# Layers 2 and 3 of a four-layer convolution chain with the image held in units of 16 rows

## Chip, core and metric

The kernel runs on one core of a Trainium2 chip. The metric is the device time in microseconds of one execution, the median of several runs. All data is float32. Engines are named as the profile names them: PE (TensorE) multiplies matrices, DVE (VectorE), ACT (ScalarE) and POOL (GpSimd) work element by element, and SP (SyncE) issues DMAs.

## The reference, cut to what matters

Four images of 192 channels and 64x64 pixels pass through four layers: a deformable convolution with channel attention and an MLP (layer 0), a non-local attention over all pixels (layer 1), an overlapping window attention with a gated MLP (layer 2), and a depthwise convolution whose weights are made from the image's mean (layer 3). The change is in layers 2 and 3:

```python
def _hft(x, w, b):
    a = 3.0 * x
    for s in (2, 4, 8):
        pool = x.reshape(B, C, h // s, s, ww // s, s).mean(axis=(3, 5))
        a = a - jnp.repeat(jnp.repeat(pool, s, axis=2), s, axis=3)
    return jax.nn.sigmoid(_dwconv3(a, w, b)) * x
...
    s_img = _reverse(s, H, W)               # sums of the softmax, folded back
    o_img = _reverse(o, H, W).reshape(B, HEADS, ch, H, W)
    out = (o_img / s_img[:, :, None]).reshape(B, C, H, W)
    out = _hft(_conv1x1(out, proj_w, proj_b), hft_w, hft_b)
    x1 = x + out
    z = jax.nn.gelu(_conv1x1(_ln_c(x1, n2g, n2b), fc1_w, fc1_b), approximate=False)
    z1, z2 = jnp.split(z, 2, axis=1)
    z = z1 * _dwconv3(_ln_c(z2, sgn_g, sgn_b), sg_w, sg_b)
    return x1 + _conv1x1(z, fc2_w, fc2_b)
...
# layer 3: weights from the mean, four of nine taps (above and left) are kept
    pooled = x.mean(axis=(2, 3))
    t = jax.nn.relu(gamma * (pooled @ w1.T - running_mean) * rsqrt(running_var + EPS) + beta)
    wt = (t @ w2.T + b2).reshape(b * DIM, 1, K, K) * MASK
    out = depthwise_conv(x, wt) + bias
```

## The kernel before, in words

The four images go through the same stages one after the other, and parts of the next image's layer 0 are woven in between.

- **Layer 0.** `offsets` (from L327; L449 computes the offsets) and `gather` (L539 to L557) do the deformable convolution; `mlp0` (L654 to L815) does the attention product and the MLP in 33 steps, four for each of eight chunks of 8 rows and one ahead. Its image is held with channels 0-127 on 128 partitions and 128-191 in halves of 64 partitions.
- **Layer 1.** `keys` (loads L826, transposes L829, products L834, copies L837) makes the keys of an image, and `layer1` (L841 to L960) is the large attention: products L881, L947. The `gather` of the next image is woven into it.
- **Layer 2, windows.** `windows` (L964 to L1182) does the attention in 8x8 windows with a stride of 6, eleven rows of eleven windows. Windows are taken in pairs. `outputs` adds each window's values into an image row by products (L1132) and, by one more product per window, the sums of the softmax (L1137): its moving operand is a piece of the identity, 64 columns.
- **Layer 2, project.** `project` (L1295 to L1359) takes the image in eight chunks of 8 rows, each as two halves of 96 channels on 96 partitions. `first(i)` does the projection (PE L1312, ACT L1315), the pooling sums by pairs (DVE L1323, L1326), their scaling (L1329), the sum of the levels (L1334), and writes a strip with a border of one pixel (ACT L1339, DVE L1345); POOL copies border rows between strips (L1266, L1267). `second(i)` does nine depthwise taps per half on DVE (L1290, L1292), a sigmoid on ACT (L1352), a product (L1354) and the add to x (L1355). For the last image five of the nine taps go to PE (L1284).
- **Layer 2, mlp.** `mlp` (L1361 to L1498) is written out by hand in a fixed order, ten iterations for eight chunks. In an iteration `widen` makes six products of 128 channels (L1387) with a gelu each (L1390), in two groups of three; the norm of the next chunk and the norm of the gate (L1398 to L1420) run between; `taps_of` does the nine gate taps of the chunk two before on DVE (two of them on PE for the last image); `narrow` multiplies back to 192 channels (L1438); `end` adds to x (L1445).
- **Layer 3.** `layer3` (L1500 to L1573) makes four weights per channel from the sums, and then for eight pieces of 8 rows and two halves each: one tap on ACT (L1562), three on DVE (L1571), a store (L1572). For the last image a part of the pieces is done on PE (L1557).
- **The weaving in `rest`.** `project`, `mlp` and `layer3` are generators. The number that each yields is added to a credit, and for each whole credit one step of the next image's `mlp0` is emitted. The yields of `project` sum to 12, of `mlp` to 19, of `layer3` to 4; 33 are used. What is left is emitted at the end. After `rest` come `keys(b+1)`, with `offsets(b+2)` woven in, and `layer1(b+1)`. For the last image there is no such neighbour. PSUM banks of tag "h" are five in `rest`, three for the last image.

Outside `mlp` a scheduler orders the instructions of each engine by its own costs, within the program's dependences. Loads and stores are issued on SP's queue in the order of the program.

Of the kernel before, what the change touches and what calls it, by code (L numbers as in the profile page):

```python
# [10 lines left out]
F32 = mybir.dt.float32  # L11
# [11 lines left out]

M, Q = 128, 64
NCH = 8
CN = HW // NCH
HN = CN // 2
HEADS = 6
# [33 lines left out]
]  # L62
_V96_ONE = ["l1_gb", "l1_thetab", "l1_phib"]
# [10 lines left out]
def conv_seq_kernel(ctx: ExitStack, tc: tile.TileContext, a, out: bass.AP):  # L74
# [22 lines left out]
    V = {}  # L97
# [10 lines left out]
    def halves_of(name, src, pool):  # L108

        t = pool.tile(list(src.shape), F32, tag=name, name=name)  # L110
        nc.sync.dma_start(out=t, in_=src)
        return t
# [24 lines left out]
    for j in range(4):  # L137
        nc.gpsimd.memset(spread[32 * j : 32 * j + 1, j, :], 1.0)
    eps = const([128, 1], "eps")
# [3 lines left out]
    for i in range(3):  # L143
# [4 lines left out]
        thetaT, phiT, gT, wW, qkvT, bias, v48, headsel, sel6, fc1_dram, fc1_bias, fc1b_dram, fc1b_bias, outb, bfc2,  # L148
    ) = (None for _ in range(15))
# [10 lines left out]
    def constants():  # L160

        nonlocal thetaT, phiT, gT, wW, qkvT, bias, v48, headsel, sel6, fc1_dram, fc1_bias, fc1b_dram, fc1b_bias, outb, bfc2
# [39 lines left out]
        bfc2 = const([M, 2], "bfc2")  # L202
        at = 2 * sum(n for _, n in _V96[: [name for name, _ in _V96].index("l0_bfc2")])
        for k, rows, to, of in ((0, P, 0, 0), (0, M - P, P, 1), (1, Q, 0, 1), (1, Q, Q, 1)):
            c = M - P if k == 1 else 0
            in_turn(nc.sync.dma_start(out=bfc2[to : to + rows, k : k + 1], in_=a["v96"][c : c + rows, at + of : at + of + 1]))
# [448 lines left out]
    def mlp0(b, m2, pool, sb, ps):  # L655
# [3 lines left out]
        fc1 = pool.tile([M, 2, 4 * C], F32, tag="fc1", name=f"fc1_{b}")  # L659
        nc.sync.dma_start(out=fc1[0:P, 0, :], in_=fc1_dram[:, 0, :])  # L660
        nc.sync.dma_start(out=fc1[P:M, 0, :], in_=fc1_dram[0 : M - P, 1, :])
        for q in range(2):
            nc.sync.dma_start(out=fc1[Q * q : Q * q + Q, 1, :], in_=fc1_dram[M - P :, 1, :])
# [94 lines left out]
        for i in range(NCH):  # L758
# [25 lines left out]
            def narrow(k):  # L784
# [11 lines left out]
                nc.vector.scalar_tensor_tensor(to, p, bfc2[:, k : k + 1], to, ALU.add, ALU.add)  # L796
# [167 lines left out]
    def windows(b, oi, load_image):  # L964
# [3 lines left out]
        with ExitStack() as s:  # L968
# [151 lines left out]
            def outputs(wr, pair, wins, v, et, sums):  # L1120
# [3 lines left out]
                for i, w in enumerate(wins):  # L1124
# [4 lines left out]
                    for e in range(3):  # L1129
# [6 lines left out]
                    pixels = ident[:, bass.ts(i, 64)].rearrange("p (r c) -> p r c", c=WS)[:, :, d0:d1]  # L1136
                    nc.tensor.matmul(  # L1137
                        to[P : P + HEADS, 0], lhsT=sums[:, pair, :], rhs=pixels, start=first, stop=last,
                        skip_group_check=True,
                    )  # L1140
# [130 lines left out]
    def depthwise(strip, w, k, diag, taps, acc, ps, name):  # L1271


        parts = strip.shape[0]

        def src(tap):
            return strip[:, k, tap // 3 : tap // 3 + 8, tap % 3 : tap % 3 + W]

        to = acc.rearrange("p (r c) -> p r c", c=W)
        last = None  # L1280
        if taps:
            p = ps.tile([128, CN], F32, tag="t", name=name)[:parts]
            for j, tap in enumerate(taps):
                nc.tensor.matmul(p, lhsT=diag[:, k, j, :], rhs=src(tap), start=j == 0, stop=j == len(taps) - 1)  # L1284
            last = p.rearrange("p (r c) -> p r c", c=W)
        for tap in range(9):
            if tap in taps:
                continue
            if last is None:
                nc.vector.tensor_scalar_mul(to, src(tap), w[:, k, tap : tap + 1])  # L1290
            else:
                nc.vector.scalar_tensor_tensor(to, src(tap), w[:, k, tap : tap + 1], last, ALU.mult, ALU.add)  # L1292
            last = to

    def project(b, x, oi, ps, taps, ahead):  # L1295


        with ExitStack() as s:
# [3 lines left out]
            hft_diag = diagonals("hft", V["l2_hftw"], 2, taps, s1) if taps else None  # L1302
            get, share = strips(s1.tile([P, 3, 2, 10, W + 2], F32, tag="hft", name=f"hft_{b}"))
            prs = {}

            def first(i):
                pr = sb.tile([P, 2, CN], F32, tag="pr", name=f"pr_{b}_{i}", bufs=3)
                prs[i] = pr
                for h in range(2):
                    p = ps.tile([128, CN], F32, tag="h", name=f"pp_{b}_{i}_{h}")[:P]  # L1310
                    for k in range(2):
                        nc.tensor.matmul(  # L1312
                            p, lhsT=projT[:, k, bass.ts(h, P)], rhs=oi[:, k, bass.ts(i, CN)], start=k == 0, stop=k == 1
                        )
                    nc.scalar.activation(pr[:, h, :], p, AF.Identity, bias=V["l2_projb"][:, h])  # L1315

                sums = [pr.rearrange("p k n -> p (k n)").rearrange("p (r c) -> p r c", c=W)]
                for lev in range(3):
# [3 lines left out]
                    t = sb.tile([P, nr // 2, ncol], F32, tag=f"pt{lev}", name=f"pt_{b}_{i}_{lev}")  # L1322
                    nc.vector.tensor_tensor(t, pairs[:, 0], pairs[:, 1], ALU.add)  # L1323
                    pairs = t.rearrange("p r (c e) -> p e r c", e=2)
                    q = sb.tile([P, nr // 2, ncol // 2], F32, tag=f"pq{lev}", name=f"pq_{b}_{i}_{lev}")
                    nc.vector.tensor_tensor(q, pairs[:, 0], pairs[:, 1], ALU.add)  # L1326
                    sums.append(q)
                for lev in range(1, 4):
                    nc.vector.tensor_scalar_mul(sums[lev], sums[lev], 0.25**lev)  # L1329
                for lev in (2, 1):  # L1330
                    fine = sums[lev].rearrange("p (r e) (c f) -> p e r c f", e=2, f=2)
                    coarse = sums[lev + 1]
                    for e in range(2):
                        nc.vector.tensor_tensor(  # L1334
                            fine[:, e], fine[:, e], coarse.unsqueeze(3).to_broadcast(list(coarse.shape) + [2]), ALU.add
                        )
                t = get(i)
                for k in range(2):
                    nc.scalar.activation(  # L1339
                        t[:, k, 1:9, 1 : W + 1], pr[:, k, :].rearrange("p (r c) -> p r c", c=W), AF.Copy, scale=3.0  # L1340
                    )
                    for e in range(2):
                        to = t[:, k, 1 + e : 9 : 2, 1 : W + 1].rearrange("p r (c f) -> p r c f", f=2)
                        mean = sums[1][:, 4 * k : 4 * k + 4, :]
                        nc.vector.tensor_tensor(to, to, mean.unsqueeze(3).to_broadcast([P, 4, 32, 2]), ALU.subtract)  # L1345
                share(i)

            def second(i):
                acc = sb.tile([P, 2, CN], F32, tag="acc", name=f"ha_{b}_{i}")
                for k in range(2):  # L1350
                    depthwise(get(i), V["l2_hftw"], k, hft_diag, taps, acc[:, k, :], ps, f"ht_{b}_{i}_{k}")
                    nc.scalar.activation(acc[:, k, :], acc[:, k, :], AF.Sigmoid, bias=V["l2_hftb"][:, k])  # L1352
                cols = bass.ts(i, CN)
                nc.vector.tensor_tensor(acc, acc, prs.pop(i), ALU.mult)  # L1354
                nc.vector.tensor_tensor(x[:, :, cols], x[:, :, cols], acc, ALU.add)  # L1355
# [414 lines left out]
```

## Time and profile before

| what | us |
|---|---|
| median of three runs | 7190.85 (7181.6 to 7196.93) |
| the profiled execution | 7273.0 |
| its span, first to last instruction | 7271.2 |
| mean granted PE clock in it | 0.921 of full |
| `windows` of the last image | 6495 to 6814 |
| `rest` of images 0, 1, 2, to the last x add or output tap | 1943 to 2502, 3650 to 4209, 5370 to 5929 |
| `rest` of image 3 | 6814 to 7267 |
| `mlp0` of image 0, with nothing beside it | 677 to 873 |

The page of the profile gives each engine's busy time, the chain of work that ended last, and the costliest groups of instructions (line, engine, operation, out<-in with partitions x elements, count; then busy time and mean ns of one; then idle time before them and what ended it). A float32 product appears as two records on PE, each with a weight load (PEld). The trace also gives the busy times of all engines between two times, which is how the stages are read; times are counted from the span's start.

### The profile page before, as it was taken

To read this page: it belongs to the slowest core of one execution; us is meant where nothing else is said; L and a number is where in the kernel's file an instruction comes from. 1 tells how busy PE (TensorE), PEld (TensorE's weight loads), DVE (VectorE), ACT (ScalarE), POOL (GpSimd) and SP (SyncE) were. 2 spreads that over 40 slices of the span, in tenths; PEclk is the share of its full clock that TensorE was granted. 3 is DMA by queue.
4 is the path that set the end of the run, shared out by engine and by line. 5 is a ranking of instruction groups with operands and counts; after the bars stand their busy time and mean duration, and the time that the engine had idled before them with its cause. 6 is when DMAs were issued, how large, how long until landed. Compare 5 with 4: busy or idle time off the path is not lost.

```text
span 7271.2 us, 117763 instructions
## 1 busy us (share of the span) xinstructions
PE 6455.8 (89%) x45792; PEld 4350.1 (60%) x45792; DVE 5104.6 (70%) x8112; ACT 3798.2 (52%) x6375; POOL 2124.8 (29%) x2412
## 2 busy tenths in 40 slices
PE   6677999999978899998978889999997889989987
PEld 3345578875544468885644448886654447766532
DVE  3554289975678759984596849995577867755767
ACT  3554278864443358874544338884443425535332
POOL 2653056742100037761200026773210000002100
PEclk8778999999989899998989889998998979989998
DMA  7785256641000176661010066763010010010000
GB/s 228 250 308 160 79 173 214 218 142 31 23 25 14 58 221 221 215 213 40 8 36 15 17 206 198 222 217 110 12 28 21 12 49 9 14 34 12 2 5 19
DMA packets 357710, 741.41 MB, mean 102 GB/s; under 512 B 45735, under 2 KB 239959, under 8 KB 356382
## 3 DMA queue, kind: packets, MB, share of 16 engines
q0 software_dynamic: 95040, 467.22, 19.9%
q1 hardware_dynamic: 262110, 266.65, 12.4%
q8 instruction: 361, 5.91, 0.3%
q14 instruction: 199, 1.63, 0.1%
HBM read 627.22 MB, written 106.21 MB: 101 GB/s over the span
## 4 chain that ended last, share of the span: by engine, by line
PE 65%; DVE 21%; ACT 4%; issue 3%; DMA 2%; SPq 1%; POOL 0%; another core or an unknown queue 0%; ACTq 0%; DVEq 0%; POOLq 0%
PE s L881 12%; PE y L947 11%; PE h L557 7%; DVE ga L1292 6%; DVE ha L1292 3%; PE v L1107 3%; PE h L1387 3%; PE qk L1032 2%; PE t L1115 2%; PE qk L1033 2%; PE f L1438 2%; PE po L449 2%; PE o L1132 1%; PE pm_l2n L327 1%; PE tp L829 1%
## 5 line engine op out<-in xcount | busy, mean ns | idle before, releaser
L539 POOL DMA_INDIRECT ring<-table,idx x1188 | 1675.6, 1410 | 1159.8 <-DVE row L546 254.5
L881 PE MATMUL s<-ths,ph 96*128 96x256 f32 x4096 | 979.4, 385 | 13.9 <-issue 9.1
L881 PEld LDWEIGHTS s<-ths,ph 96*128 96x128 f32 x4096 | 782.7, 193 | 153.6 <-issue 16.0
L545 ACT ACTIVATE row<-ring,pos 128x384 f32<-128x384 f32 x1188 | 698.5, 610 | 235.2 <-DVE xo L550 146.0
L546 DVE SCALAR_TENSOR_TENSOR row<-ring,fr,row 128x384 f32<-128x384 f32 x1188 | 699.1, 612 | 101.5 <-ACT row L545 67.6
L947 PE MATMUL y<-sc,gx 128*97 128x256 f32 x3008 | 723.4, 379 | 0.0
L549 ACT ACTIVATE xo<-row,pos 128x192 f32<-128x192 f32 x1188 | 506.2, 449 | 163.3 <-remote 57.5
L947 PEld LDWEIGHTS y<-sc,gx 128*97 128x97 f32 x3008 | 489.5, 164 | 123.1 <-issue 1.1
L1292 DVE SCALAR_TENSOR_TENSOR ga<-gate,v,ga 128x512 f32<-128x512 f32 x720 | 541.4, 752 | 28.0 <-DVE ga L1292 0.5
L550 DVE SCALAR_TENSOR_TENSOR xo<-row,fr,xo 128x192 f32<-128x192 f32 x1188 | 464.7, 411 | 134.4 <-ACT xo L549 94.6
L557 PE MATMUL h<-ti,xo 128*128 128x192 f32 x2376 | 464.7, 329 | 5.6 <-DVE xo L550 5.6
L883 ACT COPY sc<-s 128x1024 f32<-128x1024 f32 x376 | 377.2, 1003 | 172.7 <-PE s L881 144.1
L944 DVE TENSOR_TENSOR sc<-sc,mbs 128x1024 f32<-128x1024 f32 x376 | 448.7, 1217 | 12.7 <-ACT mbs L907 11.9
L888 DVE TENSOR_TENSOR top<-top,sc 128x1024 f32<-128x1024 f32 x282 | 344.5, 1222 | 137.7 <-ACT sc L883 116.6
L557 PEld LDWEIGHTS h<-ti,xo 128*128 128x128 f32 x2376 | 405.8, 191 | 42.7 <-DVE xo L550 9.9
L1091 DVE TENSOR_REDUCE es<-ex 128x6 f32<-128x384 f32 x264 | 133.3, 546 | 394.6 <-ACT ex L1087 394.6
L945 ACT ACTIVATE sc<-sc 128x1024 f32<-128x1024 f32 x376 | 393.2, 1054 | 27.3 <-DVE sc L944 18.4
L557 PE MATMUL h<-kept,xo 128*128 128x192 f32 x990 | 264.6, 403 | 123.5 <-DVE xo L550 55.7
L1387 PE MATMUL h<-d_l2n,fc1T 96*128 96x512 f32 x768 | 352.3, 607 | 10.1 <-ACT z L1390 7.8
L1266 POOL COPY gate<-gate 128x192 f32<-128x192 f32 x28 | 12.3, 440 | 1170.4 <-ACT gate L1420 1170.4
L557 PEld LDWEIGHTS h<-kept,xo 128*128 128x128 f32 x990 | 191.3, 226 | 213.3 <-DVE xo L550 85.9
L1292 DVE SCALAR_TENSOR_TENSOR ha<-hft,v,ha 96x512 f32<-96x512 f32 x432 | 304.6, 740 | 3.6 <-POOL hft L1266 2.2
(344 smaller groups left out, 11807.4 us busy)
## 6 DMA issues: line engine op xcount, KB each, us to landing
ti<-table SPq DMA_DIRECT2D x396, 96.0 KB
table<-tt SPq DMA_DIRECT2D x24, 1056.0 KB
ring<-table,idx POOLq DMA_INDIRECT x1188
xnd<-xn SPq DMA_DIRECT2D x4, 3270.0 KB
table<-kept SPq DMA_DIRECT2D x12, 1056.0 KB
table<-tt SPq DMA_DIRECT2D x44, 288.0 KB
xi<-in_x_dram SPq DMA_DIRECT2D x32, 384.0 KB
xk<-xd SPq DMA_DIRECT2D x32, 384.0 KB
```

What stands on the lines that cost most here:

```text
L539: nc.gpsimd.indirect_dma_start(out=gt.rearrange("p r q c -> p (r q c)"), out_offset=None, in_=table[:, :], in_offset=bass.IndirectOffsetOn ...
L545: nc.scalar.activation(row, gt[:, :, 0, :], AF.Copy, scale=pos[:, t, 9 + tap : 10 + tap])
L546: nc.vector.scalar_tensor_tensor(row, gt[:, :, 1, :], fr[:, t, 9 + tap : 10 + tap], row, ALU.mult, ALU.add)
L549: nc.scalar.activation(xo[:, j, :], row[:, 0, :], AF.Copy, scale=pos[:, t, tap : tap + 1])
L550: nc.vector.scalar_tensor_tensor(xo[:, j, :], row[:, 1, :], fr[:, t, tap : tap + 1], xo[:, j, :], ALU.mult, ALU.add)
L557: nc.tensor.matmul(acc[m // 2][:, bass.ts(m % 2, C)], lhsT=xo.rearrange("p j c -> p (j c)")[:, bass.ts(m, 128)], rhs=tt, start=t == 0 and ...
L881: nc.tensor.matmul(p[:, t, :], lhsT=ph[:, bass.ts(G * g + t, 128)], rhs=ths[i], start=True, stop=True)
L944: nc.vector.tensor_tensor(ex, ex, mbs[i].unsqueeze(1).to_broadcast([128, G, QN]), ALU.add)
L945: nc.scalar.activation(ex, ex, AF.Exp)
L947: nc.tensor.matmul(py, lhsT=gx[:, G * g + t, :], rhs=ex[:, t, :], start=g == 0 and t == 0, stop=g == NG - 1 and t == G - 1,)
L1292: nc.vector.scalar_tensor_tensor(to, src(tap), w[:, k, tap : tap + 1], last, ALU.mult, ALU.add)
L1387: nc.tensor.matmul(p, lhsT=fc1b[:, k, bass.ts(m, 128)], rhs=hns[i][:, k, :], start=k == 0, stop=k == 1)
```

## The change

The image of layers 2 and 3 is held as six units of 16 rows and 1024 pixels: units 0 to 3 are channels 0-127 on 128 partitions, units 4 and 5 are channels 128-191, with the upper half of the image on partitions 0-63 and the lower half on 64-127. Elementwise instructions work on a whole unit. Per-channel vectors get the same layout (`VW`), built once by 28 small products. `project` runs by unit, and its depthwise taps become a generator with yields between them. Its pooling levels are summed with a factor of 0.25 in the add, so that the scaling is gone. Between units 4 and 5 the two border rows that cross partitions are moved by DMA.

In `mlp` the chunks stay 8 rows, with 128 channels in one instruction and 64 in a second. `widen` goes over the two channel groups outside and the three outputs inside, so that three banks are open at once. `layer3` runs by unit; unit 4's row above its lower half comes by DMA (`over`). For the last image only unit 1 is on PE.

The yields change: `project` now sums to 22, `mlp` to 16, `layer3` to 0. In `windows` the softmax sums of a pair of windows are added by one product of up to 112 columns, with a constant `pixels`.

```diff
-                    pixels = ident[:, bass.ts(i, 64)].rearrange("p (r c) -> p r c", c=WS)[:, :, d0:d1]
-                    nc.tensor.matmul(
-                        to[P : P + HEADS, 0], lhsT=sums[:, pair, :], rhs=pixels, start=first, stop=last,
-                        skip_group_check=True,
-                    )
+                c0, n, m = STRIDE * wins[0] - PAD, STRIDE * (len(wins) - 1) + WS, 64 * len(wins)
+                d0, d1 = max(0, -c0), min(n, W - c0)
+                nc.tensor.matmul(
+                    pos[wr][P : P + HEADS, 0, :, c0 + d0 : c0 + d1], lhsT=sums[:m, pair, :], rhs=pixels[:m, :, d0:d1],
+                    start=wins[0] == 0, stop=wins[-1] == NWIN - 1, skip_group_check=True,
+                )
...
+    def depthwise_steps(strip, w, diag, taps, acc, ps, name):
...
+        else:
+            nc.vector.tensor_scalar_mul(acc, src(first), w[:, first : first + 1])
+        for j, tap in enumerate(others):
+            nc.vector.scalar_tensor_tensor(acc, src(tap), w[:, tap : tap + 1], acc, ALU.mult, ALU.add)
+            if j % 3 == 1:
+                yield
...
+    def upper_of(x, i):
+        q, at = i // 4, 4 * UN + CN * (i % 4)
+        rows = slice(Q * q, Q * q + Q)
+        return x[:, bass.ts(i, CN)], x[rows, at : at + CN], rows
...
+                if u == 5:
+                    nc.sync.dma_start(out=get(4)[Q:M, 0, row], in_=get(5)[0:Q, UR, row])
+                    nc.sync.dma_start(out=get(5)[0:Q, UR + 1, row], in_=get(4)[Q:M, 1, row])
...
-                for lev in range(1, 4):
-                    nc.vector.tensor_scalar_mul(sums[lev], sums[lev], 0.25**lev)
...
+            for of, u in (
+                (first, 0), (first, 1), (second, 0), (first, 2), (second, 1), (first, 4), (first, 5), (second, 4),
+                (first, 3), (second, 2), (second, 5), (None, 0), (second, 3),
+            ):
+                if of is first:
+                    first(u)
+                    yield 0.33
+                elif of is second:
+                    for _ in second(u):
+                        yield 0.83
+                else:
+                    ahead()
...
+                rows, banks = upper_of(x, i)[2], {}
+                for k, of in ((0, slice(0, M)), (1, rows)):
+                    for m in ms:
+                        if k == 0:
+                            banks[m] = ps.tile([128, CN], F32, tag="h", name=f"h2_{b}_{i}_{m}")
+                        nc.tensor.matmul(
+                            banks[m], lhsT=fc1b[of, k, bass.ts(m, 128)], rhs=hns[i][of, k, :], start=k == 0, stop=k == 1
+                        )
                 for m in ms:
-                    p = ps.tile([128, CN], F32, tag="h", name=f"h2_{b}_{i}_{m}")
-                    for k in range(2):
-                        nc.tensor.matmul(
-                            p, lhsT=fc1b[:, k, bass.ts(m, 128)], rhs=hns[i][:, k, :], start=k == 0, stop=k == 1
-                        )
...
                     if gating:
-                        yield 1.0 if last < 0 else 0.5
+                        yield 1.0 if last < 0 else 0.0
...
+            for u in (0, 1, 2, 4, 3, 5):
...
+                    rows = [(ov[:, a0:], xv[:, r0 - 1 + a0 : r0 + UR - 1])]
+                    if u == 4:
+                        rows.append((ov[:, 0:1], over))
...
+                if k == 0:
+                    nc.sync.dma_start(out=flat[0:M, bass.ts(u, UN)], in_=o)
+                else:
+                    for q in range(2):
+                        at = HW // 2 * q + UN * (u - 4)
+                        nc.sync.dma_start(out=flat[M:C, at : at + UN], in_=o[Q * q : Q * q + Q])
+                yield 0.0
-                nc.sync.dma_start(out=dst[:, :, bass.ts(i, R * W)], in_=o)
-                yield 0.5
```

## The prediction

> **What bounds the kernel now.** I read the page first, its busy shares and the chain that ended last, and then windows of the stages that the change touches.
>
> ```profile
> PE 6455.8 (89%) x45792; PEld 4350.1 (60%) x45792; DVE 5104.6 (70%) x8112; ACT 3798.2 (52%) x6375; POOL 2124.8 (29%) x2412
> ...
> PE 65%; DVE 21%; ACT 4%; issue 3%; DMA 2%; SPq 1%; POOL 0%; another core or an unknown queue 0%; ACTq 0%; DVEq 0%; POOLq 0%
> ```
>
> TensorE (PE) carries the chain as a whole, but most of it in layer 1 (L881, L947), which the change leaves alone. So I cut out the stages, by the table of windows (from:to, length, busy us of PE, PEld, DVE, ACT, POOL, then granted clock, DMA share, GB/s):
>
> ```profile
> 1943.00:2118.00 175.00, 129.54 (x513) 68.84 (x511) 165.52 (x341) 72.09 (x110) 8.44 (x30) 0.83 0.10 28
> 2118.00:2465.00 347.00, 296.74 (x1328) 155.96 (x1328) 264.25 (x371) 132.43 (x193) 9.95 (x42) 0.92 0.06 17
> 2465.00:2614.00 149.00, 131.43 (x925) 68.96 (x925) 66.36 (x101) 54.17 (x98) 11.45 (x14) 0.87 0.56 170
> 5919.00:5975.00 56.00, 55.11 (x162) 36.62 (x163) 14.39 (x24) 6.97 (x10) 3.96 (x5) 0.50 0.26 78
> 6814.00:6925.00 111.00, 107.69 (x266) 41.22 (x266) 99.65 (x220) 36.19 (x53) 12.70 (x47) 0.97 0.02 6
> 6925.00:7190.00 265.00, 219.91 (x838) 102.86 (x836) 177.33 (x224) 93.77 (x119) 10.88 (x35) 0.94 0.01 2
> 6495.00:6814.00 319.00, 289.76 (x5191) 188.70 (x5192) 169.88 (x242) 148.70 (x273) 76.48 (x195) 0.94 0.09 23
> ```
>
> Row 1 is `project` of image 0, with VectorE (DVE) busy 95%. Row 2 is its `mlp`, where neither PE (86%) nor DVE (76%) is full: it is a chain that alternates between them. Row 3 is what follows the last x add: layer 3, keys(1) and offsets(2), PE-bound. Row 4 is keys(3) after image 2, PE 98% busy but at half clock. Rows 5 and 6 are `project` and `mlp` of the last image, with no neighbour: `project` is PE-bound there. Row 7 is a `windows` stage, PE 91%.
>
> **Unit sizes on DVE.** The groups of instructions give a mean per size:
>
> ```profile
> L546 DVE SCALAR_TENSOR_TENSOR row<-ring,fr,row 128x384 f32<-128x384 f32 x1188 | 699.1, 612 | 101.5 <-ACT row L545 67.6
> ...
> L550 DVE SCALAR_TENSOR_TENSOR xo<-row,fr,xo 128x192 f32<-128x192 f32 x1188 | 464.7, 411 | 134.4 <-ACT xo L549 94.6
> ...
> L1292 DVE SCALAR_TENSOR_TENSOR ha<-hft,v,ha 96x512 f32<-96x512 f32 x432 | 304.6, 740 | 3.6 <-POOL hft L1266 2.2
> ```
>
> From 411 ns for 192 elements to 612 for 384: 1.047 ns an element and 210 ns that an instruction costs whatever its size. 512 elements come to 746 (measured 740), 1024 to 1.28 us. [...] The rows (16 x (8 x 0.740 + 0.482) = 102.4, less 6 x (8 x 1.28 + 0.80) = 66.3) make 36. The row is this kernel's own, so I take 36.
>
> **project, images 0 to 2.** DVE's own part falls from 162.8 to about 108.7 us: taps -36, pooling sums (15.4 to 11.6) -4, the scaling of L1329 -5 (folded into the adds), L1345 (13.3 to 9.0) -4, products and x adds (19.4 to 14.6) -5. Alone this would take 175 to about 125. But the new yields sum to 22 credits where the old had 12, so ten more of the 33 steps of the next image's layer-0 MLP (`mlp0`) move in: in the built order five of its eight chunks are before the first widening, not three. Priced at 0.86 us for a 512-column product (two records; the first 16 of L1312 start between 1943.2 and 1949.7 us, 0.43 apart) and half that for 64-row pairs, PE's list grows from 101 to 147.5 us. At a clock of 0.92 that is 160, with waits 167: **-8 each**. Bounds: 147.5 at 0.83, the clock of row 1, is 178 (+3); DVE's 142 plus 8 of waits is 150 (-25). The two row DMAs between units 4 and 5 wait on SyncE for unit 5's strip, and loads of mlp0 stand behind them; PE waited 2.3 us once for such a load in row 1, so a late one costs a few us, within the bounds. POOL's edge copies fall from 14 to six and POOL is idle.
>
> **mlp, images 0 to 2.** The same steps leave here. Six steady iterations, from their first spread to the next, last 36.4, 42.3, 33.6, 44.1, 33.4 us (start times of L1417; mean 38.0): the short ones carry one step of mlp0, the long ones two.
>
> ```profile
> 2206.00:2243.00 37.00, 30.91 (x133) 15.54 (x132) 31.43 (x44) 14.71 (x20) 1.58 (x4) 0.92 0.11 32
> 2243.00:2285.00 42.00, 39.66 (x189) 20.92 (x190) 32.78 (x47) 17.37 (x26) 0.78 (x4) 0.95 0.00 1
> 2285.00:2319.00 34.00, 26.88 (x116) 14.01 (x115) 32.67 (x47) 11.68 (x15) 1.53 (x4) 0.90 0.02 8
> ```
>
> In the second row PE is full, in the third DVE is. With one step each all become the third kind: 38.0 to 34.5, six times, is -21; the end gives 2 more: **-23 each**. DVE is late next, at 32.7 of 34: no removal of mlp0 can bring more than some 10 beyond this. At the other end 0 is gained if the alternation itself sets the time. mlp0 now ends at iteration 8, so keys(b+1) come among the last taps, where DVE is the bound and PE has room; if that cover is missing, eight gx copies of 0.55 us and some 25 us of PE come back. The x adds by 128 and 64 rows are as many as before.
>
> **The tail after the last x add.** Layer 3 is 18 tap instructions of 1.27 us and three short ones on DVE, about 26.5 with buffer waits, after 3.8 for the weights. All output DMAs are now ahead of the next loads on SyncE's queue, so offsets start about 34 us after the last add. Alone at the kernel's start they took 102 (5 to 107 us); I take 98, since their norms need no first loads of constants: 132 against 149, **-17** for images 0 and 1. Bounds: 68, what the part after keys took, gives -47; 102 and a cold clock give +1. After image 2 layer 1 began 83 us after the add; keys are gone, so 34, and 8 for a cold start (its first 28 us now ran at 0.74): **-41**, bounds -49 and -20.
>
> **The clock[...].** Layer 3 with nothing beside it leaves PE idle for some 25 us, and mlp has more gaps. [...] Row 4 says otherwise: 55.11 of 56 us busy, and the clock 0.50 throughout, 28 us lost. [...] by the row they lose up to 60. The start of the kernel[...] had 0.93 over its 102 us, and is nearest to a restart of the same offsets; I keep the figures above.
>
> **The last image.** project: PE's list falls by 8 (pp, 28.6 to 20.6, since the 64-row pairs run side by side) and 18 (ht, 160 records of 72.8 us to 120); DVE's falls to about 70. 111 to 84: **-27**. mlp: only three PSUM banks here, and the new widening fills three at once. In the built order the second and third wait for the x adds on DVE, which are behind a tap, not for a gelu. h3 began at 7036.3, the adds ended at 7044.2; less 3.5 of products that run meanwhile, 4.3 us in each of five iterations: **+21** (0 to +35: DVE idles 5 us there for PE anyway). Layer 3: -2. Sum -8.
>
> **windows.** 121 sums of 64 columns an image become 66, of which 55 have 112. Spacing is 0.21 us for the pair of records at 64 columns and 0.31 at 128 (L1115), so 0.29 at 112: 55 x (0.42 - 0.29) = 7 us of PE, of which 6 show at 91% busy: **-24** for four images (-38 to 0). The 28 small products of the new constants lie in the gather of image 0[...]: 0 (+4 if PE's order delays it).
>
> **Sum.** 3 x (-8 - 23) - 17 - 17 - 41 - 8 - 24 = -200. The profiled execution took 7273.0 (span 7271.2), 1.1% above the median of 7190.85; all differences are made within it. 7190.85 - 200 = **6991**.
>
> **Rivals.** *Less gain* (22%): the woven mlp is latency, not work. Its mean of 38 stays at 36.5 or so (-9 each), project stays at 175 and the keys aren't covered: -27 - 50 - 8 - 24 = about -105, **7085**. For it: neither engine is full in row 2. Against: the periods follow the number of steps. *More gain* (20%): project goes to DVE's 150 (-25 each), the mlp to DVE's 32.7 (-33 each), the tails as above: -75 - 99 - 75 - 8 - 24 = -281, **6910**. *Slower* (5%): the mlp stages, thinned of mlp0, fall to half clock and stay there, as row 4 did. PE's list there is 285 us at full clock now and about 260 after. The stage must end 74 us later than my 324 (three times) to undo the whole: 398. With 25 of waits, 260 over 373 is a clock of 0.70; below that it is slower, at 0.66 about 3 x 20 = 60 us: **7250**. Against it: row 6 is an mlp without mlp0, PE 83% busy, and its clock was 0.94. That the change does not do what it says is excluded by the built order.
>
> **Chances.** Likeliest 53% (6945 to 7040), the rivals as given. A measurement of this kernel tells about 0.2% from no change (14 us). The range takes in both milder rivals in part: 6905 to 7085. Faster 0.94, same 0.02, slower 0.04.
>
> **What would show it.** In the changed profile: `project` near 167 with PE and DVE both about 90% busy; steady mlp iterations all near 34.5; no keys after layer 3; offsets from about 34 us after the last add; the last image's mlp at some 286, with its widenings waiting for x adds. Steady iterations still at 38, or a clock below 0.75 in the second row's place, would prove me wrong.

## The result, and the profile after

The changed kernel takes 7063.4 us (median of four runs, 7056.3 to 7071.5) against 7193.9 us of the kernel before (7181.6 to 7199.6): a ratio of 0.9821, 95% interval 0.9804 to 0.9838, or -130 us. The forecast was 6991 us with a range of 6905 to 7085. A repetition gave 0.9838 (0.9811 to 0.9865).

The profiled execution took 7071.5 (span 7069.4), 202 less than that of before. Of these 202, 77 lie in the first gather, whose code the change leaves as it was: the first MLP product of image 0 (L767 before, L796 after) starts at 614 us, not 692. In all profiles here that start lies between 614 and 692 with either layout; it is late (676 to 688) in the groups of runs where the kernel before takes about 7270, and early (614 to 642) in those where it takes about 7191. So runs of different groups are compared by their ratio to before and stage by stage, and the profile of before is one of the long kind. Without those 77 the two profiles differ by 125.

The engine line of the page after is the one to set beside the first of before:

```profile
PE 6342.5 (90%) x45368; PEld 4236.5 (60%) x45368; DVE 4928.1 (70%) x7476; ACT 3763.7 (53%) x6276; POOL 2122.6 (30%) x2352
```

DVE has 636 instructions fewer and is busy 176 us less. PE is busy 113 us less.

To compare stages I use marks that both traces have: the first projection product, the first widening product, the last x add, the first theta product of the next layer 1. First the windows of before between these marks (`project` and `mlp` of image 0, `mlp` of the last image):

```profile
1943.20:2104.90 161.70, 119.44 (x495) 64.70 (x493) 153.04 (x324) 69.37 (x107) 8.44 (x30) 0.84 0.10 30
2104.90:2465.00 360.10, 306.64 (x1344) 159.91 (x1344) 276.53 (x388) 135.15 (x196) 9.95 (x42) 0.91 0.05 16
6920.30:7239.70 319.40, 247.91 (x885) 112.28 (x884) 217.12 (x283) 96.55 (x122) 10.88 (x35) 0.90 0.01 2
```

and the same three after, with `project` of the last image as the third row:

```profile
1858.60:2026.00 167.40, 158.07 (x767) 89.07 (x766) 136.45 (x206) 83.89 (x123) 5.34 (x16) 0.97 0.17 48
2026.00:2357.40 331.40, 294.44 (x1257) 141.34 (x1256) 257.68 (x365) 124.38 (x178) 12.20 (x43) 0.94 0.06 19
6549.00:6641.50 92.50, 82.38 (x213) 34.24 (x213) 65.57 (x115) 25.53 (x29) 17.10 (x36) 0.93 0.03 7
6641.50:7034.50 393.00, 299.49 (x884) 120.47 (x884) 218.99 (x287) 97.85 (x127) 6.60 (x29) 0.80 0.01 2
```

In `project` PE is now the fuller engine (158 of 167 us busy), and in `mlp` too (294 of 331). The last row is the surprise: the last image's `mlp` has as many PE instructions as before and 52 us more of PE busy time, at a clock of 0.80 instead of 0.90, and is 74 us longer.

| stage | before | after | difference | foreseen |
|---|---|---|---|---|
| project, images 0 to 2 | 161.7 each | 167.4, 166.7, 167.1 | +16 | -24 |
| mlp, images 0 to 2 | 360.2, 360.4, 360.1 | 331.4, 329.3, 327.2 | -93 | -69 |
| last x add to layer 1 | 156.6, 156.8, 82.5 | 142.4, 139.9, 35.8 | -78 | -75 |
| project, last image | 106.1 | 92.5 | -14 | -27 |
| mlp, last image | 319.5 | 393.1 | +74 | +21 |
| layer 3, last image | 31.4 | 34.8 | +3 | -2 |
| windows, four images | 1207.7 | 1192.2 | -15 | -24 |

These stages make -107. The other 18 us lie in `mlp0` and keys of image 0 (-5) and the four layer 1 stages (-13), which the change leaves alone; they were not foreseen. The border between `project` and `mlp` is a matter of the mark: before, the last x add of `project` ends 12.9 us behind the first widening product, after, 14.6 us ahead of it. What can be compared without a mark is the sum of the two: 521.9 to 522.0 before, 498.8, 496.0 and 494.3 after, so -23, -26 and -27 against the -31 foreseen.

What waits in that last `mlp`, by PE's own waits after:

```profile
PE h L1494 <- DVE x L1555: 31.5, 5, 6.3
PE f L1547 <- DVE z L1539: 31.4, 12, 5.7
PE pb_l2n L348 <- DVE r_l2n L1363: 23.5, 7, 3.9
```

The columns are the sum, how often, and the longest. The first line is new: the widening product waits for the x adds, in five iterations, 6.3 us each. That is the wait that the prediction named; but 31.5 us of waiting do not make 74. In four-us slices of one iteration, from the wait on:

```profile
6786.00:6790.00 4.00, 1.16 (x2) 0.64 (x3) 3.38 (x7) 0.00 (x0) 0.00 (x0) 0.68 0.00 0
6790.00:6794.00 4.00, 4.00 (x6) 1.36 (x5) 0.00 (x0) 0.00 (x0) 0.00 (x0) 0.50 0.01 4
6794.00:6798.00 4.00, 4.00 (x6) 1.03 (x4) 0.00 (x0) 1.37 (x2) 0.00 (x0) 0.50 0.00 0
6798.00:6802.00 4.00, 4.00 (x6) 0.99 (x5) 0.00 (x0) 0.69 (x1) 0.00 (x0) 0.50 0.00 0
6802.00:6806.00 4.00, 4.00 (x8) 1.82 (x8) 1.38 (x2) 1.26 (x2) 0.00 (x0) 0.69 0.00 0
6806.00:6810.00 4.00, 4.00 (x11) 1.56 (x10) 1.75 (x1) 1.76 (x2) 0.00 (x0) 1.00 0.00 0
```

After the wait PE is busy without a gap (4.00 of 4), and the granted clock is at 0.50 for 17.1 us (6787.4 to 6804.5). PE gets through six records in four us at first, and eleven once the clock is back. DVE and ACT stand nearly idle meanwhile, since all that they do next hangs on these products.

The five waits are alike, 6.3 us each, but what follows is not: the half clock lasts 20.5, 17.1, 20.5, 6.8 and 13.7 us. Behind the fourth wait the clock is back after four us of work:

```profile
6893.00:6897.00 4.00, 3.61 (x5) 1.27 (x5) 0.99 (x4) 0.00 (x0) 0.00 (x0) 0.54 0.00 0
6897.00:6901.00 4.00, 4.00 (x9) 1.52 (x10) 0.00 (x0) 2.06 (x3) 0.00 (x0) 1.00 0.00 0
```

The iterations with these waits last 52.0, 51.5, 53.0, 45.5 and 45.6 us; the last does less work than the others.

### The profile page after: what moved, and what is told of

Same layout as the page of the kernel before. It is cut to its first block, busy times and chain, and to the rows that moved or that the text cites. A ratio compares the mean times of both kernels' runs of the same rounds, so it can differ in the third digit from the quotient of the medians.

```text
span 7069.4 us, 116083 instructions
## 1 busy us (share of the span) xinstructions
PE 6342.5 (90%) x45368; PEld 4236.5 (60%) x45368; DVE 4928.1 (70%) x7476; ACT 3763.7 (53%) x6276; POOL 2122.6 (30%) x2352
## 4 chain that ended last, share of the span: by engine, by line
PE 45%; DVE 13%; ACT 3%; issue 2%; DMA 1%; POOL 1%; SPq 0%; DVEq 0%; ACTq 0%; POOLq 0%
PE s L910 8%; PE y L976 7%; DVE ga L1324 4%; PE h L590 3%; PE h L1494 3%; PE v L1136 2%; PE qk L1061 2%; PE qk L1062 1%; PE f L1547 1%; PE t L1144 1%; PE po L482 1%; PE zm L1506 1%; PE rb L1210 1%; PE o L818 1%; DVE top L917 1%
## 5 line engine op out<-in xcount | busy, mean ns | idle before, releaser
L572 POOL DMA_INDIRECT ring<-table,idx x1188 | 1696.2, 1428 | 1037.8 <-DMA wkT<-in_wkT_dram 234.6
L910 PEld LDWEIGHTS s<-ths,ph 96*128 96x128 f32 x4096 | 781.8, 192 | 142.4 <-ACT ths L904 16.7
L583 DVE SCALAR_TENSOR_TENSOR xo<-row,fr,xo 128x192 f32<-128x192 f32 x1188 | 465.5, 412 | 40.6 <-ACT xo L582 38.1
L1494 PE MATMUL h<-d_l2n,fc1T 128*128 128x512 f32 (+1 forms) x768 | 375.5, 630 | 34.0 <-DVE x L1555 31.5
L1297 POOL COPY gate<-gate 128x192 f32<-128x192 f32 x28 | 13.9, 497 | 1286.0 <-ACT gate L1528 1286.0
L1494 PEld LDWEIGHTS h<-d_l2n,fc1T 128*128 128x128 f32 (+1 forms) x768 | 143.6, 197 | 252.8 <-issue 189.2
L1547 PE MATMUL f<-z,fc2T 128*64 128x512 f32 (+1 forms) x384 | 222.6, 714 | 74.1 <-DVE z L1539 74.1
```

The source lines that it names most:

```text
L572: nc.gpsimd.indirect_dma_start(out=gt.rearrange("p r q c -> p (r q c)"), out_offset=None, in_=table[:, :], in_offset=bass.IndirectOffsetOn ...
L583: nc.vector.scalar_tensor_tensor(xo[:, j, :], row[:, 1, :], fr[:, t, tap : tap + 1], xo[:, j, :], ALU.mult, ALU.add)
L910: nc.tensor.matmul(p[:, t, :], lhsT=ph[:, bass.ts(G * g + t, 128)], rhs=ths[i], start=True, stop=True)
L1494: nc.tensor.matmul(banks[m], lhsT=fc1b[of, k, bass.ts(m, 128)], rhs=hns[i][of, k, :], start=k == 0, stop=k == 1)
```

## The experiments

Theory 1: the gain of some 200 us is there, less what the last image's `mlp` loses to the wait and to the half clock that it brings. Rivals: the split into 128 and 64 channels costs the time itself; the gain comes from the yields alone and the layout does nothing; the tails are set by the clock.

**Old order of the widening, last image only.**

```diff
-                for k, of in ((0, slice(0, M)), (1, rows)):
-                    for m in ms:
+                both = ((0, slice(0, M)), (1, rows))
+                order = [(k, of, m) for m in ms for k, of in both] if taps else [(k, of, m) for k, of in both for m in ms]
+                for k, of, m in order:
+                    if True:
```

> The changed kernel, with the old order of the widening products (each output's two products together) for the last image only; the other three images keep the new order. Theory 1: the last image's mlp became 74 us longer (319 to 393) because the second and third bank wait for the x adds (6.3 us in each of five iterations) and because PE then runs at half clock for 15 to 20 us (7.7 us more). Both go: mlp about 320, total about 6993. Rival: the 128 + 64 split of norms, adds and products costs the time by its own instructions; mlp stays above 380, total 7050 to 7065.

Measured: 0.9795 (0.9770 to 0.9819); the last `mlp` took 346.6 us, with steady iterations of 40.6 us (52.0, 51.5, 53.0 and 45.5 in the changed kernel, 37.9 before). The wait for the x adds is gone. So the order of the loops is the cause of most of the 74. But 27 us remain against before. The old order has a price of its own, as the PE timeline shows; first this run, then the run below, which keeps the new order. Columns: start, time from the first start to the last end, engine and line, group.

```profile
6864.52 6.29 PE L1496 MATMUL h<-d_l2n,fc1T 128*128 128x512 f32 x12
```

```profile
6828.41 5.51 PE L1494 MATMUL h<-d_l2n,fc1T 128*128 128x512 f32 x12
```

Twelve records take 6.29 us against 5.51. From start to start of two records the trace of the changed kernel has 0.43 us where the records have the same number of rows and come in a row, 0.52 at a change of the number of rows, from 128 to 64 or back, and 0.53 for a second record right behind a change. The new order makes one change of height per three outputs, the old one five. Over the stage the widening products keep PE busy 102.5 us with the old order, 89.9 in the run below and 87.9 before: some 13 to 15 of the 27. Where the rest lies is open. The old order also has the wait of before for a free bank:

```profile
PE h L1496 <- ACT z L1500: 7.8, 10, 0.8
```

**The x adds ahead of the first tap, last image only.**

```diff
+                    if taps:
+                        end()
                     if last >= 0:
                         taps_of(last, 0)
                     end()
```

> The changed kernel, but for the last image the x adds are emitted ahead of the first gate tap of the iteration instead of behind it; the widening keeps its new order. Theory 1: the wait of PE falls from 6.3 us to 2 or less[...], so mlp falls from 393 to about 320 to 330, total about 6995 to 7005. Rival (the split itself costs the time): no change, 7063. If the order of the two loops cost something else than this wait, this run stays clearly above the one with the old order.

Measured: 0.9766 (0.9741 to 0.9791); the last `mlp` 323.1 us, steady iterations 37.3. PE's waits in that stage:

```profile
PE f L1547 <- DVE z L1539: 27.1, 12, 4.5
PE pb_l2n L348 <- DVE r_l2n L1363: 23.5, 7, 3.9
PE pb_z L348 <- DVE rz L1596: 4.6, 1, 4.6
```

The line `PE h <- DVE x` is gone, and with it 70 us of the stage, with all the split instructions in place. The rival that the split costs the time is out. The whole moved by 0.0055 of 7194, some 40 us, not 70. It ran in another group than the changed kernel, one with the longer first gather, and its own layer 1 of image 0 was 19 us longer in the profile; with intervals of 12 and 18 us each way, where the other 30 went stays open.

**Work in the place of the wait.**

```diff
                             banks[m] = ps.tile([128, CN], F32, tag="h", name=f"h2_{b}_{i}_{m}")
+                            for _ in range(7 if taps and m == 3 and 2 < i else 0):
+                                nc.tensor.matmul(
+                                    banks[m], lhsT=fc1b[of, k, bass.ts(m, 128)], rhs=hns[i][of, k, :], start=True, stop=True
+                                )
```

> The changed kernel, and for the last image seven more products with the same operands into the bank of the first output, ahead of the real one, in iterations 3 to 7: about 6 us of work in the place where PE waits. The wait for the x adds stays what it is. If the half clock after the wait costs 7.7 us an iteration as the trace suggests, the period falls from 51 to about 43.5 and the total by about 39, to 7025, although work is added. If the clock is only a symptom and costs nothing on the path, the period stays at 51 and the total at 7063.

Measured: 0.9792 (0.9765 to 0.9818), the stage 360.3 us, steady iterations 43.9 where 43.5 was expected. The same place in an iteration, behind the x adds at 6855.7:

```profile
6852.00:6856.00 4.00, 4.00 (x10) 1.52 (x8) 3.79 (x6) 0.00 (x0) 0.00 (x0) 1.00 0.00 0
6856.00:6860.00 4.00, 3.71 (x9) 1.53 (x9) 1.07 (x4) 0.46 (x1) 0.00 (x0) 1.00 0.00 0
6860.00:6864.00 4.00, 4.00 (x9) 1.27 (x8) 0.64 (x1) 1.60 (x3) 0.00 (x0) 1.00 0.00 0
6864.00:6868.00 4.00, 4.00 (x10) 1.71 (x9) 2.50 (x3) 1.33 (x3) 0.00 (x0) 1.00 0.00 0
```

The clock is 1.00 throughout these 16 us. The five iterations last 44.2, 43.9, 43.9, 43.9 and 39.6 us, so six us of useless products made them shorter by 7.8, 7.6, 9.1, 1.6 and 6.0: least where the changed kernel had its short half-clock stretch of 6.8 us. Added work that shortens an iteration, and most where the half clock was longest, leaves the clock as the only cause. By the whole stage, the clock is 33 us (393.1 to 360.3) and the wait itself 37 (360.3 to 323.1).

**The window sums alone, on the kernel before.** The diff is the part of the change above in `outputs`, with its constant.

> The kernel before, with only the sums of a pair of windows by one product of up to 112 columns (and its constant). Prediction's term: 6 us an image, -24, about 7168. From the trace of the changed kernel: PE's busy time in a windows stage falls by about 12 us at equal clock, but in three of four of its windows stages there is a half-clock stretch of 20 us that before did not have. If this stretch comes with the change of the sums: -10 to -20 in all, about 7178; if not: -40 to -50, about 7148.

Measured: 0.9946 (0.9928 to 0.9964), -39 us, at the upper of the two ends. A windows stage of it, beside 298.1 us and 280.26 of PE before:

```profile
1639.60:1928.40 288.80, 266.40 (x5028) 176.92 (x5027) 165.92 (x235) 144.97 (x268) 70.08 (x192) 0.96 0.10 27
```

PE has 110 records less and 13.9 us less to do, where the prediction had 7. The next rows give the PE and PEld time of the sums alone (first two) and of the value products alone (last two) in that stage, each time before and then this run:

```profile
1645.10:1943.20 298.10, 33.12 (x242) 11.40 (x242) 0.97 0.10 26
1639.60:1928.40 288.80, 22.20 (x132) 6.17 (x132) 0.96 0.10 27
1645.10:1943.20 298.10, 39.48 (x1452) 20.39 (x1452) 0.97 0.10 26
1639.60:1928.40 288.80, 27.58 (x1452) 17.00 (x1452) 0.96 0.10 27
```

(The two kinds overlap in time, so their gains do not add up to 13.9.) So about half of the gain is in products that are as many as before. The likely reason, not tested apart, is that the 64-row value products of two windows now follow each other, where a sum with 128 rows stood between: in the trace of the kernel before, a value product starts 0.15 us behind such a sum (54 times in this stage at full clock), and in that of the changed kernel 0.02 behind the value products of the window ahead. The sums themselves were priced well: from the starts of its records a product of 112 columns takes 0.29 us, one of 64 columns 0.21.

The -39 cannot all be put to this, though. The two profiles differ by 52 us; 35 lie in the windows stages, and 17.6 in the tail of image 2, which this edit leaves alone (its half clock lasted 23.9 us instead of 68.3). And the rival of the expectation came true in the stages: in 31 of the 48 windows stages that were traced with the new sums, a half-clock stretch of 20.5 us or so begins 41 to 43 us into the stage, in none of the eight with the old sums, of which one has a stretch of 54.6 us. With it the new stages take 299.1 us on the mean, without it 291.3, the old ones 297.0 without that one. So the stretch eats most of what the sums save, and their worth lies somewhere between almost nothing and 39 us. It disturbs the pair of profiles above, which shows -15.

**Layout without the yields, and yields without the layout.** In the first, the changed kernel has `yield 0.18` and `0.455` in `project`, 0.5 in `mlp`, 0.667 in `layer3`; in the second, the kernel before has `yield 0.917` and `1.833`, 0.0 and 0.0.

> The changed kernel with its yields scaled to the old sums (project 12, mlp 19, layer 3 four), so that the next image's layer-0 MLP and keys lie where they lay before. Theory: the layout alone frees DVE in project, and the yields move the freed place to the tails. Then project falls to about 131 (from 167), the woven mlp goes back to about 360 (from 331), and the tails come back (78 us in three): together +57 against the changed kernel, ratio 0.990. Rival: the layout is the gain and the yields only shift it about: ratio stays at 0.982.

> The kernel before with only its yields changed to the new sums (project 22, mlp 16, layer 3 none), on the old layout. Theory: project becomes longer (PE's list 154 us over DVE's 163: about 185, +23), mlp shorter by 29, the tails by about 60 in three: -78 in all, ratio 0.989. Rival: without the lighter DVE of the new layout project grows by all that it takes in (+65 each), and the ratio is 1.01 or more.

Measured: 0.9875 (0.9835 to 0.9915) for the layout with the old yields, 0.9913 (0.9885 to 0.9941) for the new yields on the old layout; the changed kernel in the same group 0.9838. `project` and `mlp` of image 0, first with the layout alone:

```profile
1858.40:1988.40 130.00, 110.05 (x495) 60.34 (x493) 116.29 (x177) 60.01 (x85) 4.61 (x16) 0.89 0.13 38
1988.40:2349.30 360.90, 316.39 (x1348) 155.24 (x1344) 272.36 (x384) 138.99 (x204) 9.92 (x42) 0.93 0.05 16
```

then with the yields alone:

```profile
1899.20:2095.80 196.60, 165.30 (x765) 90.96 (x765) 179.77 (x365) 92.40 (x145) 7.13 (x30) 0.93 0.14 41
2095.80:2419.50 323.70, 282.82 (x1237) 145.28 (x1237) 253.59 (x353) 121.84 (x171) 12.15 (x42) 0.92 0.06 16
```

The layout alone takes `project` from 161.7 to 130.0, where DVE is busy 116, and leaves `mlp` as it was. The yields alone make `project` 35 longer and `mlp` 36 shorter, and take 8.4, 8.8 and 38 off the tails. In images 0 and 1 the three stages together are 639 us with the layout alone and 636 to 641 in the changed kernel: with the layout, moving steps from `mlp` into `project` only exchanges the one for the other, since PE is nearly full in both. All that the yields add to the layout is the tail of image 2 (76.2 to 35.9), where keys are the whole of what follows. Against the changed kernel of the same group the three stages make +37, not the +57 of the expectation: the tails of images 0 and 1 came back by 8 us each, not 17.

**PE kept busy in layer 3.**

```diff
+                if not alone:
+                    p = ps.tile([128, CN], F32, tag="h", name=f"warm_{b}_{u}")
+                    for j in range(4):
+                        nc.tensor.matmul(p, lhsT=ident, rhs=o[:, 0:CN], start=True, stop=True)
```

> The changed kernel, with four products that nobody reads after each unit of layer 3 in the first three images, on the unit just finished: PE is busy where it idled some 25 us. In the trace of the changed kernel half clock lasts 44, 44 and 38 us from the start of layer 3, some 20 to 30 of it over the following offsets or layer 1. If PE's idleness causes it: -10 to -13 in each tail, -35 in all, ratio 0.977. If the half clock came with the kind of work (it stood at 0.50 for 56 us of busy PE before): no change, 0.982.

Measured: 0.9824 (0.9795 to 0.9854), no different from the changed kernel. The half-clock stretch at the start of the tails of images 0 and 1 fell from 44 us to two of 14, so PE's idleness is the cause of most of it; but the tails were 144.1, 143.0 and 40.1 instead of 139.7, 139.7 and 35.8. The added products are themselves some 21 us of PE a tail (48 records), so a small gain from the clock could hide behind them; none shows. What the tail waits for is in PE's waits of the changed kernel there:

```profile
PE pm_l L360 <- DMA xi<-in_x_dram: 30.5, 1, 30.5
PE th L902 <- DMA xc<-xd: 6.8, 1, 6.8
```

One load of the next offsets comes 30 us late. It reads the kernel's input, which is there from the start; it stands on SyncE's queue behind the stores of layer 3, and these wait for DVE:

```profile
SPq L1696 <- DVE out L1694: 24.5, 4, 15.7
```

**Later steps of mlp0.** The x adds first as above, and `yield 1.0 if last < 0 else -0.5` in iterations 2 to 7.

> The changed kernel with the x adds first for the last image, and with half a step of the next image's layer-0 MLP less in each of iterations 2 to 7 of mlp: its last steps come in iterations 8 and 9, and keys fall beside layer 3, where PE idles some 25 us. Theory: keys are free there, mlp loses 6 x 1.5 us of PE, the tails grow little: -10 to -40 against adds_first, ratio 0.971 to 0.975. Rival: the end of mlp was the free place, and keys beside layer 3 wait for their loads behind the stores: +5 to +20 in each tail, ratio 0.98.

Measured: 0.9794 (0.9770 to 0.9817). The three `mlp` fell to 322.6, 323.0, 322.7 (-5 to -8 against adds first), the tails rose to 157.8, 158.6 and 55.3 (+16 to +20 each). The size is the rival's: the end of `mlp`, where DVE has its taps, is the better place for keys. Its reason, that keys wait for loads behind the stores, is not shown: the longest wait for a load of keys was 6.3 us here, and 6.4 in the run with the x adds first.

**The x adds first in all images, and the old order in the woven ones.** The first has `end()` ahead of the taps for all; the second has the old order of the widening for images 0 to 2, and the x adds first for the last.

> The changed kernel with the x adds first in all four images. The three woven images have five banks and no wait of PE for the adds in the trace, so there: no gain (0 to -5 each); the last image -70 as in adds_first. Ratio 0.975 to 0.977. If DVE's order matters for the gate taps that follow: mlp of the first three images longer than 331.

> The changed kernel with the x adds first for the last image, which keeps the new order of the widening products; the first three images get the old order, each output's two products together. From the run with the old order in the last image: start to start 0.43 us between records of equal height, 0.52 from 128 to 64 rows, 0.94 from 64 to 128, and 0.53 within an alternating pair: 14.7 us for the 24 records of an iteration instead of 11.5, 3.2 x 8 = 26 us of PE an image. If PE sets mlp's time: 331 to about 350 and +60 in all against adds_first, ratio 0.985. If the mlp is DVE or latency: no change, 0.977.

Measured: 0.9770 (0.9741 to 0.9798) and 0.9766 (0.9731 to 0.9800). The totals tell nothing apart, the stages do: the woven `mlp` takes 336 to 340 us with the adds first, and 337 with the old order, against 328 to 330. Adds first costs DVE's taps some 9 us an image where there was no wait to remove. The changes of height cost 7 to 8 us an image. The 26 us of the expectation were mispriced: 0.94 us from 64 rows to 128 is a mean that took in the waits of 0.8 us for a free bank. In the woven stages of this run all of these changes take 0.52, which makes 0.78 us for twelve records and 12.5 an image.

**The stores on another queue.** The x adds first for the last image, and in `layer3`:

```diff
-                    nc.sync.dma_start(out=flat[0:M, bass.ts(u, UN)], in_=o)
+                    (nc.sync if alone else nc.gpsimd).dma_start(out=flat[0:M, bass.ts(u, UN)], in_=o)
...
```

The stores of units 4 and 5 are changed in the same way.

> The changed kernel with the x adds first for the last image, and with layer 3's stores of the first three images issued by POOL instead of SyncE. In the changed kernel's tails PE waited 30 us for the first load of the next offsets, and that load stands on SyncE's queue behind the stores, which wait for DVE. Theory: the loads now come at once; in images 0 and 1 the offsets' first differences still queue behind layer 3 on DVE, so the tails shrink by some 10 us (140 to 130); after image 2 nothing else holds layer 1, and its tail falls from 36 to about 12. In all -45 against adds_first, ratio 0.970. Rival: the loads were late for another reason (buffers, or DVE's layer 3 sets the tail): tails within 3 us of 140 and 36, ratio 0.977.

Measured: 0.9725 (0.9699 to 0.9750), the lowest ratio here, though its interval overlaps that of the x adds alone. The tails fell to 137.0, 133.5 and 7.3 us, from 142.1, 138.9 and 35.7 with the x adds alone. The theory holds in its place, and its size is about half: PE's waits from the last x add of image 0 on are now

```profile
PE pv_l L339 <- ACT sq_l L367: 27.9, 3, 27.1
```

so the load comes at once, the first mean is made, and then the norm waits 27 us for its square on ACT, which stands behind layer 3 on DVE and ACT. After image 2 layer 1 begins 29 us earlier, and its own length grows from 543 to 558, for the same reason:

```profile
PE s L910 <- ACT ths L904: 15.9, 1, 15.9
```

## Why the prediction was right, and where its terms were off

The direction and the range held; 70 of the 200 us did not come. The 7063 lies outside the likeliest band (6945 to 7040), nearer to the number of the rival with less gain (7085), but not for that rival's reasons: the wide range caught what its middle missed. Some luck is in it too: without the 18 us that came from stages the change leaves alone, the miss would be 90.

- **project and mlp, woven: "-8" and "-23" each.** The 167 for `project` held up to the first widening product (167.4, 166.7, 167.1, PE 94% busy). But the 175 from which it was taken off ran to the last x add of `project`, 13 us behind that product; to the same mark it was 161.7, so the term is +5.5. Those 13 us come back in `mlp`, which gave -29, -31 and -33. Together they gave 23 to 27 of the 31. The iterations were foreseen well on the mean: the five that the prediction lists (it calls them six) went from 38.0 to 35.1, 34.7 and 34.4 us, against 34.5. They did not become alike, as it said, but still range from 30 to 38. PE is now busier than DVE (294 and 258 of 331); which of them sets the time is not shown, since adds first for all left PE's work as it was and cost 9 us.
- **DVE's saving.** 1.28 us for a tap of 1024 elements was taken from two rows; 1.275 was measured. DVE's own part of `project` fell from 162.8 to 106.3 us, 108.7 foreseen. With the old yields, so with as many steps of mlp0 beside it as before, `project` up to its last x add is 38 us shorter (174.6 to 136.3), less than the 50 that this was to bring.
- **The tails: "-17, -17, -41".** -14, -17, -47. Right in size and in reason, the late loads: the first offsets product comes 38 us after the last add, 34 foreseen. The half clock of row 4, by which the prediction put a loss of up to 60 us in all on the tails, decided nothing here: with 44 us of it brought down to two stretches of 14, the first tail took 144.1 us instead of 139.7.
- **The last image's mlp: "+21".** +74. The wait was named, in its place and on its five iterations, at 4.3 us; it was 6.3. The sum took off 3.5 us of products that run meanwhile, and only the two records of one product run, 1.0 us. The failed step is that I stopped at the wait, with nothing for the clock behind it; I had weighed the clock only for the tails. Here it is 33 of the 74 us. After the waits of 1.8 to 4.6 us in the first eight iterations the half clock lasted 3.4 to 6.8 us, after those of 6.3 it lasted 6.8 to 20.5, through unbroken work. What it cost an iteration, DVE and ACT waiting along, is 1.6 to 9.1 us by the run with the wait filled. Row 4 of the prediction (0.50 for 56 busy us) had warned of it.
- **project of the last image: "-27".** -14. To the same marks PE's busy time fell by 20.5 us (102.9 to 82.4), not 26: the projection products went from 28.6 to 24.6, not to 20.6 (the pairs of 64 output channels do run side by side, their two records starting 0.01 us apart and the 32 of them busy 7.1 us, but the 32 records of 128 channels took 17.5 us, not 32 x 0.43), the depthwise products by 17.4 as foreseen. And PE now waits where the prediction had no wait, above all for the strip of unit 4:

```profile
PE ht L1318 <- DMA x<-x: 7.4, 1, 7.4
```

  In the run with the stores on another queue the wait at this place is 7.2 us and ends with DVE (L1444), so the row DMAs between units 4 and 5 by themselves add little to it.
- **windows: "-24".** -15 between the two profiles, -39 by the run of this part alone. The price of 0.29 us for 112 columns was right, though 44 products have as many, not 55. The sum left out the cheaper value products on one side and the half-clock stretch on the other, and that the two nearly cancel was not foreseen.
- **The slower rival**, a clock that falls in the thinned `mlp`, came true only in the last image, by another way: not by thinness but by one wait per iteration. In the woven images the clock was 0.94.
- The terms of the rival with less gain add up to -109, not to the -105 that stands there; nothing hangs on it.

## What to carry to other kernels

A wait on PE is priced by its length plus what the clock does after it: here 37 us for the five waits and 33 for the half clock behind them. Where an added wait like the 6.3 us here comes back every iteration, look at the granted clock behind it before pricing it, and look first for an order in which the engine never stands that long: the x adds ahead of the taps took this stage from 393.1 to 323.1 us. Before moving work from one stage to another, add up the fuller engine over both: where it is nearly full in both, as PE is here (158 of 167 us and 294 of 331), the move brought next to nothing: 636 to 641 us for the three stages after it, 639 without it. Measure both sides of a comparison to the same mark: a stage on DVE can end 13 us behind the mark on PE. A load that needs nothing from a stage should not be queued behind that stage's stores: here it came 30 us late, and with the stores on POOL's queue the tail of image 2 fell from 35.7 to 7.3 us, though the layer 1 after it grew by 15.

## What the runs showed of the hardware

- In the traces of the kernel before and of the changed one, 182 of the 184 half-clock stretches last 3.4, 6.8, 10.2, 13.7, 17.1, 20.5 us and so on: multiples of 3.4. Five waits of PE of 6.3 us were followed by stretches of 20.5, 17.1, 20.5, 6.8 and 13.7 us, with PE busy behind each wait; useless products in the place of the wait kept 1.00. Why the clock took two to six times 3.4 us to come back is open.
- In the changed kernel PE pays for a change between 128 and 64 rows from one float32 record of 512 columns to the next: 0.52 us from start to start instead of 0.43, in both directions, and 0.53 for a second record right behind it. A change between 96 and 128 rows, in the kernel before, kept 0.43.
- One kernel can differ by some 80 us between groups of runs, most of it, by the profiles, in the first gather by indirect DMA (the first product behind it starts at 614 to 692 us), so that a difference of profiles from two groups is not a difference of kernels until the stages are compared. What makes the gather longer in some groups is open.
